# A four-layer convolution kernel on one core: keys transposed into single banks, four copies of x ahead of their products, the first load in halves, and layer 2's outputs of the second pair made two at a time

## The chip, the core and the metric

The kernel runs on one core of one Trainium2 chip, in one launch. The metric is the device time of that launch in microseconds; the median of several runs counts. TensorE (PE) multiplies matrices and writes into PSUM, which has eight banks of 128 partitions by 512 float32 values. VectorE (DVE) and ScalarE (ACT) work on what lies in PSUM and in the on-chip memory, GpSimd (POOL) does little here, and SyncE (SP) issues nearly all transfers (DMA). Each engine works through its own list in order, and semaphores make one engine wait for another.

## The reference

Input x has the shape (4, 512, 64, 64) in float32; four layers follow each other. Cut to what matters:

```python
# layer 0: attention over the 4096 places, 64 channels wide
t = einsum('oc,bchw->bohw', w_qkv, x)          # key, query, value: 64 rows each
attn = softmax(einsum('bdk,bdq->bkq', key, query), axis=1)
x = scale * einsum('oc,bchw->bohw', w_out, value @ attn) + x
# layer 1: three convolutions (1x1, 3x3, 1x1) with weights mixed from 8 experts, relu, plus x
# layer 2: linear attention
Q, K = softplus(Wq x + bq), softplus(Wk x + bk)          # 64 features at each place
KV = einsum('bmn,bcn->bmc', K, Wv x + bv)
norm = 1 / einsum('bnm,bm->bn', Q, K.sum(-1) + EPS)
x = x + gamma * einsum('bnm,bmc,bn->bcn', Q, KV, norm)
# layer 3: two 1x1 projections; one is summed with a discount along rows and columns
x = x + gamma * x_gate * sigmoid(cumsum(cumsum(x_scan, rows), columns))
```

## The kernel before

The four batches run one after the other, and within a batch the layers. A batch's x (512 channels, 4096 places) lies in four "pairs" of 1024 places (two blocks of 512), each a tile of 128 partitions by 4 groups of channels by 1024. PE's order is the program's order; DVE's and ACT's order is partly written by hand too (`manual_schedule`). PSUM is shared out by two pools: `pair_psum` gives two banks as one tile and has three such places, `bank` gives a single bank and has two. A tile can be written when the tile that stood in its place before has been read.

A float32 matmul shows as two records in the trace. Products with 64 rows or 64 columns of weights are issued for both halves of a pair, and their records run side by side.

**Start.** `load_pair` (line 87) loads the first batch's x on SP's queue, one transfer of 512 KB for each group of channels; the weights of layer 0's projections (`wqkv_sb`, line 99) come in two halves, one on ACT's queue, one first on SP's (line 102). Meanwhile PE makes two products of the identity with itself, the step "zero" (lines 305 to 310), and then the first products of x (`vv`, line 269), both halves of the pair.

**Layer 2.** `features` makes the key's features, `softplus` turns them into keys (logarithm on ACT, lines 701 to 717 on DVE). `key_transpose` (line 720) turns two pairs' keys by eight transposes into one `pair_psum` tile (`ktr`) and copies it with one instruction (`kt`, line 726). `move` (line 743) turns a quarter of a pair's x by eight transposes (`xtr`, line 748) and copies it out (`xt`, line 750) on ACT or DVE; `products` (line 755) multiplies keys and x into `g` (line 761). For the first pair the order is: quarters 0 and 1 moved early, keys turned, quarters 2 and 3 moved, the products of quarters 0 and 1, two moves of the next pair, the products of quarters 2 and 3 (`split=True`). After the second pair's products comes `kfold` (line 886), which needs the sums of all keys.

**Layer 3.** A batch's eight blocks (a pair and half of the channels) are made from lists of steps (lines 1118 to 1140): "s5" and the like are PE products for the sums, "g5" for the gates of the block before, the other words are work of ACT and DVE. Among them stand the outputs of layer 2 for pairs 1 to 3, twelve of them, in a list `ys`: "y" makes the next one (`value_product`, line 926, two products of 64 rows, `wv` at line 930), "a" adds it to x on DVE (`value_add`, line 935). "q" takes the next piece of what is left of layer 2 for the last two pairs from the list `left`: features, the sums' product `den2` (line 856, a bank) with its reciprocal on DVE (line 859), and `divide` (line 862, PE line 866, DVE line 869).

Of the kernel before, what the change touches and what calls it, by code (L numbers as in the profile page):

```python
# [14 lines left out]
B, C, H, W = 4, 512, 64, 64  # L15
P = 128
HW = H * W
NB = 512
# [3 lines left out]
D = 64  # L22
NT = HW // P
TPB = NB // P
NPAIR = NBLK // 2
# [21 lines left out]
def unshifted(ctx: ExitStack, tc: tile.TileContext, fits, x, wqkv_t, wout_t, router_t,  # L47
# [38 lines left out]
    def load_pair(b, pr):  # L86
        if b and pr == NPAIR - 1:
            places[NPAIR - 1:] = places[NPAIR], places[NPAIR - 1]
        t = places[pr]
        src = x[b, :, pr * 2 * NB:(pr + 1) * 2 * NB].rearrange("(kc p) n -> p kc n", p=P)  # L90
        if b == 0:
            for kc in range(KC):
                nc.sync.dma_start(t[:, kc, :], src[:, kc, :])
        else:
            nc.sync.dma_start(t, src)
        return t
# [1 line left out]

    wqkv_sb = const.tile([P, KC, 3 * D], F32, tag="wqkv", name="wqkv_sb")

    for queue, k in ((nc.scalar, 0), (nc.sync, 2)):
        queue.dma_start(wqkv_sb[:, k:k + 2, :], wqkv_t[:, k:k + 2, :])
    prm_sb = const.tile([P, NPRM], F32, tag="prm", name="prm_sb")
    def col(i, n=1):
        return prm_sb[:, i:i + n]
# [113 lines left out]
    class Projections:  # L219
# [70 lines left out]
        def products(self, xs, pair, steps, key, qry, vt):  # L290
            y = zy = None
            e = {}

            def to_key(src, pr, own=True):
                for h in range(2):
                    n0 = (2 * pr + h) * NB
                    for to in range(2):
                        if own or to != h:
                            nc.scalar.copy(key[to * D:(to + 1) * D, n0:n0 + NB], src(h, n0))

            for step in steps:
                step, _, channels = step.partition(":")
                if y is None and (step.isdigit() or step == "zero"):
                    y, zy = bank(f"kq_{self.b}_{pair[0]}"), pair_psum(f"kqz_{self.b}_{pair[0]}")
                if step == "zero":


                    for _ in range(2):
                        nc.tensor.matmul(zy[:, 0, :].rearrange("p (j c) -> p j c", c=P), ident,
                                         ident[:, None, :].to_broadcast([P, TPB, P]), start=True, stop=True)  # L310
                elif step.isdigit():
                    k = int(step)
                    to = y if k in (1, 6, 7, 4) else zy[:, 0 if k == 2 else 1, :]
                    for c in (int(channels),) if channels else range(2):
                        for h in range(2):
                            nc.tensor.matmul(to[h * D:(h + 1) * D, :], self.w[k][:, c, :],  # L316
                                             self.term(xs, pair, k, c)[:, h * NB:(h + 1) * NB],
                                             start=c == 0 and k in (1, 5), stop=c == 1,
                                             skip_group_check=k not in (1, 5))
                elif step == "roots":  # L320
                    norm_roots()
                elif step == "factors":
                    norm_factors()
                elif step == "seed":
                    nc.scalar.copy(zy[:, 0, :], y)
                elif step in ("e2", "e3"):
                    e[step] = block(f"{step}_{self.b}_{pair[0]}")
                    nc.scalar.copy(e[step], y)
                elif step == "c11":
                    to_key(lambda h, n0: zy[h * D:(h + 1) * D, 0, :], pair[0])  # L330
                elif step == "c12":
                    for h in range(2):
                        r, n0 = slice(h * D, (h + 1) * D), (2 * pair[1] + h) * NB
                        nc.vector.tensor_tensor(key[r, n0:n0 + NB], zy[r, 1, :], e["e2"][r, :], ALU.add)
                    self.left.append(lambda: to_key(lambda h, n0: key[h * D:(h + 1) * D, n0:n0 + NB], pair[1],
                                                    own=False))
                elif step == "k":
                    self.key_copies()
                elif step == "c21":
                    nc.vector.tensor_copy(qry[:, pair[0] * NB:(pair[0] + 1) * NB], y)  # L340
                elif step == "c22":
                    nc.vector.tensor_tensor(qry[:, pair[1] * NB:(pair[1] + 1) * NB], zy[:, 1, :], e["e3"], ALU.add)
                elif step[0] in "tn" and step[1].isdigit():
# [326 lines left out]
    def layer2(b, xs, sums_of_six, mix_last, conv2, conv3, wcq, qs):  # L670
# [47 lines left out]
                    kts[w, pr] = None  # L718

        def key_transpose(pair):  # L720
            ktr = pair_psum(f"ktr_{b}_{pair[0]}")
            for i, pr in enumerate(pair):
                for j in range(TPB):
                    nc.tensor.transpose(ktr[:, i, j * P:(j + 1) * P], kts[1, pr][:, j * P:(j + 1) * P], ident)
            kt = four(f"kt_{b}_{pair[0]}")
            nc.vector.tensor_copy(kt, ktr)
            for i, pr in enumerate(pair):
                kts[pr] = kt[:, i, :].rearrange("p (j c) -> p j c", c=P)

# [13 lines left out]
        def move(pr, j):  # L743
# [3 lines left out]
                for kc in range(KC):  # L747
                    nc.tensor.transpose(xtr[:, h, kc * P:(kc + 1) * P], xs[pr][:, kc, n0:n0 + P], ident)  # L748
# [6 lines left out]
        def products(pr, more=range(TPB), between=None, split=False):  # L755
            def multiply(js):
                for j in js:
                    t = pr * TPB + j
                    xt = moved.pop(0)
                    for h in range(2):  # L760
                        nc.tensor.matmul(g[h * D:(h + 1) * D, :], kts[pr][:, j, h * D:(h + 1) * D], xt[:, h, :],  # L761
                                         start=t == 0, stop=t == NPAIR * TPB - 1)
# [197 lines left out]
    def layer3(b, xs, value_product, value_add, left, weights, wcq):  # L960
# [109 lines left out]
        class Gates(Block):  # L1070
# [32 lines left out]
            def add_x(self, i, h=None):  # L1103
# [37 lines left out]
        with tc.manual_schedule(engines={mybir.EngineType.DVE, mybir.EngineType.Activation}):  # L1141
# [9 lines left out]
            for i in range(len(tiles) + 1):  # L1151
                who = {"l": last, "s": Sums(1, i) if i < len(tiles) else None, "g": Gates(0, i - 1) if i else None}
                if b == B - 1 and i >= len(tiles) - 1:
# [1 line left out]
                        break  # L1155
                    who["h"] = Gates(0, i)
                    who["h"].last = True
                made = None
                for step in first_steps if i == 0 else end_steps if "h" in who else steps if who["s"] else last_steps:
                    for what in step:  # L1160
                        name, *args = what.split()
# [3 lines left out]
                        elif name in who:  # L1165
                            if who[name]:
                                getattr(who[name], args[0])(*[int(a) for a in args[1:]])
                        elif name == "y":
                            if ys:
                                made = ys.pop(0)  # L1170
                                y = value_product(*made)
                        elif name == "a":
                            if made:
                                value_add(*made, y)
                                made = None
# [487 lines left out]
```

## Time and profile before

| | |
|---|---|
| median of 5 runs | 2639.87 us (2639.17 to 2640.45) |
| the profiled execution: time, span from first to last instruction | 2640.41 us, 2638.6 us |
| busy: DVE, ACT, POOL | 2066.2, 1320.5, 12.7 us |
| granted TensorE clock, mean | 0.999 |
| PE's share of the chain that ended last | 98% |
| DMA, mean over the span | 44 GB/s |

A row of the timeline gives the start, the duration, the engine, the line, what is written from what, the shapes, how many equal instructions are merged in the row, and in brackets how long the engine had been idle and what ended that. Since a matmul's end is modelled, starts are compared rather than durations. A row of the chain of waits gives the start, the time that the piece takes on the chain, and what it is.

### The profile page before, as it was taken

To read this page: it belongs to the slowest core of one execution; us is meant where nothing else is said; L and a number is where in the kernel's file an instruction comes from. 1 tells how busy PE (TensorE), PEld (TensorE's weight loads), DVE (VectorE), ACT (ScalarE), POOL (GpSimd) and SP (SyncE) were. 2 spreads that over 40 slices of the span, in tenths; PEclk is the share of its full clock that TensorE was granted. 3 is DMA by queue.
4 is the path that set the end of the run, shared out by engine and by line. 5 is a ranking of instruction groups with operands and counts; after the bars stand their busy time and mean duration, and the time that the engine had idled before them with its cause. 6 is when DMAs were issued, how large, how long until landed. Compare 5 with 4: busy or idle time off the path is not lost.

```text
span 2638.6 us, 25820 instructions
## 1 busy us (share of the span) xinstructions
PE 2626.3 (100%) x10018; PEld 1115.6 (42%) x10018; DVE 2066.2 (78%) x2332; ACT 1320.5 (50%) x1523; POOL 12.7 (0%) x26
## 2 busy tenths in 40 slices
PE   9999999999999999999999999999999999999998
PEld 3333455344333345444433334544443333554443
DVE  7777876888777787688877778768887777876887
ACT  4564353454555436345556553635555555263545
POOL 1000000000000000000000000000000000000000
PEclk9999999999999999999999999999999999999999
DMA  5000210022200021012220002101121000210001
GB/s 194 1 1 1 104 32 1 30 97 80 80 0 1 1 104 32 1 50 78 80 80 1 1 1 104 32 0 64 64 86 74 1 1 12 93 33 1 32 40 57
DMA packets 34739, 115.16 MB, mean 44 GB/s; under 512 B 3120, under 2 KB 12080, under 8 KB 33072
## 3 DMA queue, kind: packets, MB, share of 16 engines
q1 hardware_dynamic: 34464, 113.23, 11.4%
q8 instruction: 80, 1.31, 0.2%
q14 instruction: 51, 0.42, 0.1%
q10 hardware_dynamic: 144, 0.20, 0.0%
HBM read 79.86 MB, written 33.55 MB: 43 GB/s over the span
## 4 chain that ended last, share of the span: by engine, by line
PE 98%; DVE 1%; DMA 0%; ACT 0%; issue 0%; SPq 0%; ACTq 0%
PE av L399 17%; PE s L384 17%; PE sx L1012 16%; PE zy L1012 12%; PE c L657 4%; PE c L585 4%; PE c L634 3%; PE wv L930 3%; PE y L443 2%; PE g L761 2%; PE vv L269 2%; PE z L682 2%; PE kq L316 2%; PE xtr L748 2%; PE kqz L316 2%; PE c2e L634 2%
## 5 line engine op out<-in xcount | busy, mean ns | idle before, releaser
L384 PE MATMUL s<-qv,key 64*128 64x512 f32 x2048 | 454.0, 593 | 0.0
L387 ACT ACTIVATE ring<-s 128x1024 f32<-128x1024 f32 x336 | 315.4, 1053 | 249.9 <-PE s L384 249.9
L392 DVE TENSOR_TENSOR acc<-acc,ring 128x1024 f32<-128x1024 f32 x312 | 381.6, 1223 | 50.5 <-ACT ring L387 21.9
L399 PE MATMUL av<-ring,qv 128*64 128x512 f32 x1344 | 301.5, 595 | 0.0
L384 PEld LDWEIGHTS s<-qv,key 64*128 64x128 f32 x2048 | 192.7, 186 | 254.0 <-issue 112.4
L1012 PE MATMUL sx<-t,x 128*128 128x512 f32 x512 | 232.4, 594 | 0.0
L392 DVE TENSOR_TENSOR acc<-acc,x 128x1024 f32<-128x1024 f32 x168 | 205.5, 1223 | 32.4 <-ACT x L387 16.6
L387 ACT ACTIVATE x<-s 128x1024 f32<-128x1024 f32 x176 | 166.8, 1056 | 127.3 <-PE s L384 127.3
L399 PEld LDWEIGHTS av<-ring,qv 128*64 128x64 f32 x1344 | 92.6, 137 | 200.1 <-issue 200.1
L1017 ACT COPY zy<-sx 128x512 f32<-128x512 f32 x64 | 36.5, 570 | 253.9 <-PE sx L1012 253.9
L399 PE MATMUL av<-x,qv 128*64 128x512 f32 x704 | 159.5, 595 | 0.0
L1062 DVE TENSOR_TENSOR_SCAN t<-x,t 128x512 f32<-128x512 f32 x128 | 149.2, 1209 | 1.6
L1012 PEld LDWEIGHTS sx<-t,x 128*128 128x128 f32 x512 | 96.7, 190 | 124.6 <-issue 120.7
L1021 ACT ACTIVATE e<-sx,prm_sb 128x512 f32<-128x512 f32 x128 | 87.8, 686 | 122.2 <-PE sx L1012 122.2
L1045 DVE TENSOR_TENSOR_SCAN s<-wc,s 128x512 f32<-128x512 f32 x128 | 146.0, 1202 | 0.0
L1051 ACT COPY t<-s 128x1024 f32<-128x1024 f32 x64 | 127.5, 1992 | 29.2 <-DVE s L1045 28.7
L1068 ACT ACTIVATE s<-t 128x1024 f32<-128x1024 f32 x64 | 125.8, 1991 | 11.2 <-DVE t L1062 11.1
L1012 PE MATMUL zy<-t,wq 128*128 128x512 f32 x256 | 118.5, 602 | 0.0
L1012 PE MATMUL zy<-x,wq 128*128 128x512 f32 x256 | 118.0, 600 | 0.0
L1012 PE MATMUL sx<-x,wq 128*128 128x512 f32 x256 | 117.1, 595 | 0.0
L1012 PE MATMUL sx<-t,wq 128*128 128x512 f32 x256 | 116.6, 595 | 0.0
L1012 PE MATMUL zy<-x,x 128*128 128x512 f32 x256 | 116.3, 594 | 0.0
(262 smaller groups left out, 3506.4 us busy)
## 6 DMA issues: line engine op xcount, KB each, us to landing
out_dram<-s SPq DMA_DIRECT2D x62, 512.0 KB, 2.6
x<-in_x_dram SPq DMA_DIRECT2D x12, 2048.0 KB, 8.6
x<-in_x_dram SPq DMA_DIRECT2D x16, 512.0 KB, 9.1
ex<-in_packed_dram SPq DMA_DIRECT2D x4, 2048.0 KB, 8.2
ex<-in_experts_dram SPq DMA_DIRECT2D x4, 2048.0 KB, 7.7
wq<-in_wproj_t_dram SPq DMA_DIRECT2D x32, 256.0 KB, 4.7
ex<-in_packed_dram SPq DMA_DIRECT2D x4, 1536.0 KB, 6.0
ex<-in_experts_dram SPq DMA_DIRECT2D x4, 1536.0 KB, 6.4
```

The source lines that it names most:

```text
L316: nc.tensor.matmul(to[h * D:(h + 1) * D, :], self.w[k][:, c, :], self.term(xs, pair, k, c)[:, h * NB:(h + 1) * NB], start=c == 0 and k in ...
L384: nc.tensor.matmul(s[:, h, :], key[r, kt * P:(kt + 1) * P], qry[r, pr * NB:(pr + 1) * NB], start=True, stop=True)
L387: nc.scalar.activation(p, s, AF.Exp)
L392: nc.vector.tensor_tensor(accs[pr], accs[pr], p, ALU.add)
L399: nc.tensor.matmul(avs[pr][h * D:(h + 1) * D, :], vt[:, kt, :], ring[i % RING][:, h, :], start=kt == 0, stop=kt == NT - 1)
L585: nc.tensor.matmul(y[:, h, :], wc[:, kc, :], xs[pr][:, kc, h * NB:(h + 1) * NB], start=kc == 0, stop=kc == KC - 1)
L634: nc.tensor.matmul(y[:, lo - a:hi - a], u, v[:, lo:hi], start=dy == 1, stop=dy == 2)
L1012: nc.tensor.matmul(y, w[:, c, self.kind, self.j * P:(self.j + 1) * P], v[:, c, :], start=c == 0 and k in (1, 5), stop=c == 1, skip_group_c ...
L1045: nc.vector.tensor_tensor_scan(self.half(i, h), along[:, self.j + 2 * i, :], self.half(i, h), 0.0, ALU.mult, ALU.add)
L1051: nc.scalar.copy(self.t[i].rearrange("p (w r) -> p w r", w=W), self.s[i].rearrange("p (r w) -> p w r", w=W))
L1062: nc.vector.tensor_tensor_scan(th, down[:, i, :], th, 0.0, ALU.mult, ALU.add)
L1068: nc.scalar.activation(self.s[i].rearrange("p (r w) -> p w r", w=W), tw, AF.Sigmoid)
```

## The change

Four things are changed.

- Start: the first x transfer is split into two halves by columns and goes first on SP's queue; the second half of the weights follows it. The first of the two products of the identity is half as wide.
- Keys of the first two pairs: each is turned into a single bank and copied out by an instruction of its own.
- x of the first pair: quarters 2 and 3 are moved, then all four quarters are multiplied, then the second pair's four quarters are moved and multiplied. `g` takes its bank after the keys. The copies of quarter 3 (pair 0) and quarter 2 (pair 1) change places between ACT and DVE.
- Layer 3's first block: "y" becomes "yy", two outputs in a row, at two places, so that all four outputs of pair 1 are made there. Later blocks draw from the same list, and an output of pair 2 or 3 isn't made while `left` holds anything.

```diff
@@ load_pair
-                nc.sync.dma_start(t[:, kc, :], src[:, kc, :])
+                if (pr, kc) == (0, 0):
+                    for h in range(2):
+                        nc.sync.dma_start(t[:, kc, h * NB:(h + 1) * NB], src[:, kc, h * NB:(h + 1) * NB])
+                    nc.sync.dma_start(wqkv_sb[:, 2:4, :], wqkv_t[:, 2:4, :])
+                else:
+                    nc.sync.dma_start(t[:, kc, :], src[:, kc, :])
...
-    for queue, k in ((nc.scalar, 0), (nc.sync, 2)):
-        queue.dma_start(wqkv_sb[:, k:k + 2, :], wqkv_t[:, k:k + 2, :])
+    nc.scalar.dma_start(wqkv_sb[:, 0:2, :], wqkv_t[:, 0:2, :])
@@ step "zero"
-                    for _ in range(2):
-                        nc.tensor.matmul(zy[:, 0, :].rearrange("p (j c) -> p j c", c=P), ident,
-                                         ident[:, None, :].to_broadcast([P, TPB, P]), start=True, stop=True)
+                    for n in (TPB // 2, TPB):
+                        nc.tensor.matmul(zy[:, 0, 0:n * P].rearrange("p (j c) -> p j c", c=P), ident,
+                                         ident[:, None, :].to_broadcast([P, n, P]), start=True, stop=True)
@@ key_transpose
-            ktr = pair_psum(f"ktr_{b}_{pair[0]}")
+            if pair[0] == 0:
+                ktr = [bank(f"ktr_{b}_{pr}") for pr in pair]
+            else:
+                ktr = pair_psum(f"ktr_{b}_{pair[0]}")
...
-            nc.vector.tensor_copy(kt, ktr)
+            if pair[0] == 0:
+                for i in range(2):
+                    nc.vector.tensor_copy(kt[:, i, :], ktr[i])
+            else:
+                nc.vector.tensor_copy(kt, ktr)
@@ move
-            (nc.scalar.copy if j % 2 or (pr > 1 and j) else nc.vector.tensor_copy)(xt, xtr)
+            (nc.scalar.copy if pr and j else nc.vector.tensor_copy)(xt, xtr)
@@ products
-            if split:
-                multiply((0, 1))
-                for j in range(2):
-                    move(pr + 1, j)
-                multiply((2, 3))
-            else:
-                multiply(range(TPB))
+            for j in range(TPB):
+                t = pr * TPB + j
+                xt = moved.pop(0)
...
@@ layer 2, first two pairs
-            g = bank(f"g_{b}", (P, C))
             last_keys = features(1, (2, 3))
             keys()
             rest()
             key_transpose((0, 1))
+            g = bank(f"g_{b}", (P, C))
             move(0, 2)
+            move(0, 3)
             keys = last_keys()
-            products(0, (3,), split=True)
-            keys()
-            products(1, (2, 3))
+            products(0, ())
+            products(1, between=keys)
@@ layer 3
-                       ("s7", "s copy_out 3", "s fourth", "y"), ("s4", "s third", "a", "d"), ("y", "a", "q"),
+                       ("s7", "s copy_out 3", "s fourth", "yy"), ("s4", "s third", "a", "d", "a"), ("yy", "a", "a", "q"),
...
-                            if ys:
-                                made = ys.pop(0)
-                                y = value_product(*made)
+                            while ys and len(made) < len(name) and not (ys[0][0] > 1 and left):
+                                at = ys.pop(0)
+                                made.append((*at, value_product(*at)))
...
-                                value_add(*made, y)
-                                made = None
+                                value_add(*made.pop(0))
```

More of the change, by code (lines that the diff above doesn't have):

```diff
@@ L720, in key_transpose @@
         def key_transpose(pair):
-            ktr = pair_psum(f"ktr_{b}_{pair[0]}")
+            if pair[0] == 0:
+                ktr = [bank(f"ktr_{b}_{pr}") for pr in pair]
+            else:
+                ktr = pair_psum(f"ktr_{b}_{pair[0]}")
             for i, pr in enumerate(pair):
                 for j in range(TPB):
-                    nc.tensor.transpose(ktr[:, i, j * P:(j + 1) * P], kts[1, pr][:, j * P:(j + 1) * P], ident)
+                    to = ktr[i] if pair[0] == 0 else ktr[:, i]
+                    nc.tensor.transpose(to[:, j * P:(j + 1) * P], kts[1, pr][:, j * P:(j + 1) * P], ident)
             kt = four(f"kt_{b}_{pair[0]}")
-            nc.vector.tensor_copy(kt, ktr)
+            if pair[0] == 0:
[3 more added lines that the diff above has]
+                nc.vector.tensor_copy(kt, ktr)
             for i, pr in enumerate(pair):
@@ L749, in move, with products @@
             xt = four(f"xt_{b}_{pr}_{j}")
-            (nc.scalar.copy if j % 2 or (pr > 1 and j) else nc.vector.tensor_copy)(xt, xtr)
+            (nc.scalar.copy if pr and j else nc.vector.tensor_copy)(xt, xtr)
             moved.append(xt)
[L755 to L762, printed above, removed]
+        def products(pr, more=range(TPB), between=None):
             for j in more:
@@ L768, in products @@
                     between = None
-            if split:
-                multiply((0, 1))
-                for j in range(2):
-                    move(pr + 1, j)
-                multiply((2, 3))
-            else:
-                multiply(range(TPB))
+            for j in range(TPB):
+                t = pr * TPB + j
+                xt = moved.pop(0)
+                for h in range(2):
+                    nc.tensor.matmul(g[h * D:(h + 1) * D, :], kts[pr][:, j, h * D:(h + 1) * D], xt[:, h, :],
+                                     start=t == 0, stop=t == NPAIR * TPB - 1)
         with tc.manual_schedule(engines={mybir.EngineType.DVE}):
@@ L1157, in layer3 @@
                     who["h"].last = True
-                made = None
+                made = []
                 for step in first_steps if i == 0 else end_steps if "h" in who else steps if who["s"] else last_steps:
@@ L1167, in layer3 @@
                                 getattr(who[name], args[0])(*[int(a) for a in args[1:]])
-                        elif name == "y":
-                            if ys:
-                                made = ys.pop(0)
-                                y = value_product(*made)
+                        elif name in ("y", "yy"):
+                            while ys and len(made) < len(name) and not (ys[0][0] > 1 and left):
+                                at = ys.pop(0)
+                                made.append((*at, value_product(*at)))
                         elif name == "a":
                             if made:
-                                value_add(*made, y)
-                                made = None
+                                value_add(*made.pop(0))
                         elif name == "q":
```

## The prediction

> **What bounds the kernel.** The page first: PE is taken to be busy over the whole span, and the chain that ended last is 98% PE.
>
> ```profile
> PE 2626.3 (100%) x10018; PEld 1115.6 (42%) x10018; DVE 2066.2 (78%) x2332; ACT 1320.5 (50%) x1523; POOL 12.7 (0%) x26
> ```
>
> So only what takes time out of PE's own list counts. The waits of PE alone show how little there is to be had by waiting less:
>
> ```profile
> PE xtr L748 <- DVE kt L726: 1.8, 4, 0.4
> ...
> PE vv L269 <- DMA x<-in_x_dram: 0.2, 1, 0.2
> ```
>
> The first is one wait in each batch, at the place that the change rebuilds. But a busy PE isn't one at its pace. The chain in order of time, layer 3, first batch:
>
> ```profile
> 565.80 6.87 PE sx L1012 x16
> 592.35 6.87 PE sx L1012 x16
> 616.38 6.87 PE sx L1012 x16
> ```
>
> Sixteen records take 6.87 us, so 0.43 each. A block with two outputs of layer 2 in it takes 592.35 - 565.80 = 26.55 us, one without 616.38 - 592.35 = 24.03. An output thus costs (26.55 - 24.03) / 2 = 1.26 us. Its four records run two by two, 2 x 0.43 = 0.86 us, so 0.40 us goes into leaving the 128-row products and coming back. The chain of the first block shows where:
>
> ```profile
> 462.56 1.91 PE sx L1012 x4
> 464.47 1.06 PE wv L930 x4
> 465.53 0.98 PE den L856 x4
> 466.51 1.91 PE zy L1012 x4
> ```
>
> The output takes 1.06 instead of 0.86, and four records right after one take 1.91 instead of 1.72. Two outputs in a row take 1.92 (at 444.95 in the same view), that is 1.72 + 0.20: the second costs its 0.86 alone. Now layer 2, PE's timeline (start, duration):
>
> ```profile
> 405.05 1.04 PE L748 MATMUL xtr<-ident,x 128*128 128x128 f32 x8
> 406.53 1.09 PE L748 MATMUL xtr<-ident,x 128*128 128x128 f32 x8 [0.45 <-DVE kt L726]
> 407.55 1.94 PE L761 MATMUL g<-xt,kt 128*64 128x512 f32 x8
> 409.42 1.97 PE L748 MATMUL xtr<-ident,x 128*128 128x128 f32 x16
> 411.32 1.94 PE L761 MATMUL g<-xt,kt 128*64 128x512 f32 x8
> 413.18 1.97 PE L748 MATMUL xtr<-ident,x 128*128 128x128 f32 x16
> ```
>
> Quarter 3 of x starts 1.48 us after quarter 2, where eight transposes need half of 413.18's sixteen, 0.87 to 0.95: it waits for a place in PSUM that the keys hold until DVE's copy ends at 406.48. And the start:
>
> ```profile
> 1.46 3.78 PE L309 MATMUL kqz<-ident 128*128 128x512 f32 x4 [1.46 <-POOL ident masks.py:199]
> 5.43 1.97 PE L269 MATMUL vv<-x,wqkv_sb 128*64 128x512 f32 x4 [0.19 <-DMA x<-in_x_dram]
> 7.16 1.15 PE L316 MATMUL kq<-x,wqkv_sb 128*64 128x512 f32 x4
> ```
>
> Four records side by side take 1.73 us here and 0.86 from 8.13 on: PE runs at half pace until some 7.4 us.
>
> **Layer 2, the change costed.** Base: this execution's 2640.41 us (span 2638.6, 1.8 around it); the median of the runs, 2639.87, is 0.54 lower. The keys no longer hold a pair's place, and what stood in the three places before is read by then, so quarter 3 follows quarter 2 at 405.92. The keys' banks were last read by ACT's two half copies, done at 400.64, and `g` waits for the first keys' copy, which its products need anyway: both cost nothing. So the wait and its restart go, and the products start at 406.89 instead of 407.55: 0.66 gained. Not splitting removes one crossing into the 64-column products and back. Products and moves between 407.55 and 415.08 hold 16 records two by two (3.43) and 32 transposes at 0.109 (1.90 for sixteen at 413.18, less half a crossing; 3.49), 6.92 of 7.53, so two crossings cost 0.61 and one 0.30. Per batch 0.66 + 0.30 = 0.96, four times 3.85.
>
> What could take it back, step by step in before's clock. DVE is free of the query's features at 405.16; two copies of 0.69 (512 wide, as L713's and L340's rows) replace one of 1.23 and end at 405.9 and 406.5, so the products at 406.89 have their keys. DVE then copies quarter 2 to 407.7 and, new to it, quarter 3 to 408.85; the products ask for them at 408.7 and 409.5. Behind that copy stands L701, ending at 409.4 instead of 408.2, and behind it ACT's logarithm (408.24, now 409.5). Nobody misses it: the move of the next pair's first quarter starts at 410.47, its copy on DVE (1.13 after the start, as at 409.42 and 410.55) runs 411.6 to 412.85 and the fourth move, which takes its place, asks at 413.15. Then L708, L709 and two L713 follow as before (4.84 us from that copy's start to the last accumulation, 410.55 to 415.39) and end at 416.45. The products of the second pair run 414.1 to 417.6; `kfold` asks at 417.7. ACT, idle 2.24 and 1.78 us ahead of its copies, takes quarter 2 of the second pair; its last copy waits for L709 (415.1), ends at 416.15, and is asked for at 416.7. The smallest cover is 0.3 us. Bounds per batch: 1.0 if all holds, 0.35 if a new wait as long as the old one (0.6) appears; I take 0.96, since every step has cover.
>
> **Layer 3.** Before, block 0 and 1 hold four outputs in four crossings; after, [two], [two], and block 1 has one, since at its first "y" `left` still holds `divide`. The list then runs out in block 5 with one output instead of two. So twelve outputs cross 10 times, not 12: 2 x 0.40 = 0.80 us per batch without waits. But the second "yy" needs PSUM places that DVE frees by the first two adds. DVE's rows:
>
> ```profile
> 463.97 1.22 DVE L935 TENSOR_TENSOR x<-wv,x 128x1024 f32<-128x1024 f32 x1
> 465.58 1.22 DVE L935 TENSOR_TENSOR x<-wv,x 128x1024 f32<-128x1024 f32 x1 [0.39 <-PE wv L930]
> 466.72 3.34 DVE L859 RECIPROCAL inv<-den 64x512 f32<-64x512 f32 x1
> ```
>
> First pair 461.43 to 463.35 (1.92), "s4" 1.91, third output at 465.26: the first add ends at 465.19, just in time. The fourth output could start at 466.22; two adds in a row take 2.36 (at 446.06), so the second ends at 466.33: 0.16 late with its handover, and I add 0.10 for the restart, half of a crossing. Behind it `den2` moves from 465.46 to 467.43, and the reciprocal, which now follows two more adds, from 466.72 to 468.72, ending at 472.06. Before, block 1's first gate product waited for that bank (PE's next rows start at 468.26 and, eight records later, at 472.03: 3.77 where 3.44 + 0.09 is the pace, 0.24 lost); after, it could start at 471.95 and starts at 472.11, with its restart 0.26 lost, 0.03 with rounding more than before. DVE's next work (scans, 4.55 us) moves by 2.0 while PE moves by 0.8; the add that stood after the scans (1.19) is gone, and 2.45 us of DVE idle before L1076 covers the rest. Gain 0.80 - 0.26 - 0.03 = 0.51 per batch, 2.04 in all. Bounds: 0.80 without the wait, 0 if waits eat it; I take 0.51.
>
> **Start.** Half a product of the identity less is 0.86 us: PE is free at 4.4. The weights landed 3.4 us after their issue at 0.75, the first x (512 KB) 4.1 after 1.20, so 512 KB took 1.2 us behind the weights' 192. The first half (256 KB where 192 stood) lands at an estimated 4.3, the second 0.65 later at 4.95. One side of the products starts at 4.4, the other at 5.0, against 5.43; at half pace these 0.4 to 1.0 us are worth 0.2 to 0.5. I take 0.35. SP issues one more transfer (0.42), and the second pair's first x, ninth in line now, is issued only after a landing (4.1), which costs nothing while the four before it are still on their way (DVE's row at 11.04 is the first to use it); the later weights land at about 5.4; they are first read by PE at 10.7 and by DVE's short sums from 4.14 (2.6 us, ahead of idle until 11.04). DVE's first difference of x, whose halves end at 12.26 and 13.48, is asked for at 13.31 and 14.17, so up to 0.6 may be gained before it binds. Bounds: a gain of 0.9 if the pace rises earlier too; a loss of 3.0 if a pause before x makes PE start its 5.9 us of half pace again. I hold to the middle, since a pause of 0.19 did no harm.
>
> [...]
>
> **The sum.** 3.85 + 2.04 + 0.35 = 6.24 us: 2634.2 for the profiled execution, 2633.6 for the median.
>
> **Rivals.** (1) The pairs gain nothing: waits on the adds eat all. For it: the fourth output is late by my own count, and the third has only 0.05 in hand. Against it: one late start costs 0.26, and 0.80 is at stake. 2639.87 - 3.85 - 0.35 = 2635.7. (2) The pairs never wait: 2639.87 - 3.85 - 3.20 - 0.35 = 2632.5. For it: DVE's handovers are as short as 0.05. (3) The layer-2 part doesn't do what it says: the wait only moves, to quarter 3's copy or the fourth move (0.3 us of cover). Gain there 0.36 per batch: 2636.0. (4) The start loses its pace: 2633.6 + 0.35 + 3.0 = 2637.0. (5) Slower: DVE arrives late in layer 3's first block by the copy it took over (1.22) and puts both new adds (2.36) ahead of the reciprocal, on which the first gate product waits. Each batch loses 3.58 and gains 0.96 + 0.80: 4 x 1.82 - 0.35 = +6.9, 2646.8. It decides from a lateness of 1.6 us per batch on. Against it: DVE idles 6.62 us ahead of L918 and 1.50 ahead of L708, after which it runs in step with PE.
>
> **How the numbers follow.** A measurement of this kernel tells about 0.2%, 5.3 us, from no change. Forecast 0.60 (2633.0 to 2634.5), (2) 0.12: faster 0.72. (1) 0.13, (3) 0.06, (4) 0.03: within 0.2%, 0.22. (5) and its like 0.06. The range runs from 2631.7 (all upper bounds, 4.0 + 3.2 + 0.9 = 8.1) to 2637.0 (rival 4).
>
> **What would show it.** PE's wait on `kt` gone and `kfold` 0.96 us nearer to the keys' features; one row of 16 products for each pair; `wv` x8 in block 0 with at most one short wait before the fourth output; PE's first gate product after L859; block 5 1.26 us shorter; x products from 4.4 to 5.0. I am wrong if PE's waits name `xt`, L935 or L859 with more than 0.3 us per batch, or if the pace rises later than 7.4.

## The result and the profile after

The changed kernel takes 2634.10 us (median of 23 runs, 2633.01 to 2636.08); beside it on the same chips the kernel before takes 2639.69 us (43 runs, 2638.79 to 2641.64). That is 5.59 us less, a ratio of 0.9979 with a 95% interval of 0.9974 to 0.9985. The profiled execution took 2634.01 us, its span is 2632.2 us: 6.4 less than the span before.

The page of the changed kernel, busy time by engine, and all waits of PE that the trace lists (total in us, how often, longest). Most lines of the code are four further down than before (L1016 was L1012, L934 was L930), those of layer 2's transposes and products more (L733 was L724, L761 was L748, L778 was L761):

```profile
PE 2621.2 (100%) x10018; PEld 1117.0 (42%) x10018; DVE 2065.3 (78%) x2336; ACT 1321.1 (50%) x1523; POOL 12.1 (0%) x26
```

```profile
PE kqz L313 <- POOL ident masks.py:199: 1.5, 1, 1.5
PE vv L273 <- DMA x<-in_x_dram: 0.6, 1, 0.6
PE vv L273 <- DMA wqkv_sb<-in_wqkv_t_dram: 0.3, 1, 0.3
PE kqz L320 <- DVE ring L265: 0.2, 1, 0.2
```

The wait on `kt`, four times 0.45, is gone, and the list names no wait in its place in layers 1 to 3. What is new or longer in it lies in the first 15 us. DVE has four copies more (2336 instead of 2332), PE the same 10018 records.

PE's timeline in layer 2, first batch (start, duration, and so on, as before):

```profile
404.23 1.09 PE L733 MATMUL ktr<-ident,k 128*128 128x128 f32 x8
405.16 1.91 PE L761 MATMUL xtr<-ident,x 128*128 128x128 f32 x16
407.00 3.65 PE L778 MATMUL g<-xt,kt 128*64 128x512 f32 x16
410.58 3.71 PE L761 MATMUL xtr<-ident,x 128*128 128x128 f32 x32
414.22 3.65 PE L778 MATMUL g<-xt,kt 128*64 128x512 f32 x16
417.81 0.39 PE L890 MATMUL kfold<-ks,fold 128*128 128x4 f32 x2
```

Quarters 2 and 3 are one row of sixteen transposes without a pause, and each pair's products are one row of sixteen. From the first turned key to `kfold` it is 417.81 - 404.23 = 13.58 us; before it was 0.97 more, 418.67 - 404.12, by these two rows:

```profile
404.12 1.09 PE L724 MATMUL ktr<-ident,k 128*128 128x128 f32 x8
418.67 0.39 PE L886 MATMUL kfold<-ks,fold 128*128 128x4 f32 x2
```

The chain of waits in order of time (start, time on the chain, what), layer 3 of the first batch, its first block and the places where the blocks repeat:

```profile
460.64 1.92 PE wv L934 x8
462.56 1.91 PE sx L1016 x4
464.48 2.17 PE wv L934 x8
466.65 0.98 PE den L860 x4
...
565.69 6.87 PE sx L1016 x16
...
590.98 6.87 PE sx L1016 x16
...
615.01 6.87 PE sx L1016 x16
```

The first two outputs take 1.92 us and the second two 2.17: the fourth waited 0.25. The block from 565.69 to 590.98 takes 25.29 us with one output in it; before it was 26.55 with two.

Both traces laid side by side at the same rows of PE say where the time went. At the first key transposes of the batches the changed kernel is +0.11, -1.66, -3.15, -4.64 us against before; at `kfold` -0.86, -2.62, -4.11, -5.60; at PE's last product -6.12. So:

| part | forecast, us | in the profile, us |
|---|---|---|
| layer 2, four batches | -3.85 | -3.85 (-0.97, -0.96, -0.96, -0.96) |
| layer 3, four batches | -2.04 | -2.13 (-0.55, -0.53, -0.53, -0.52) |
| start, up to the first key transposes | -0.35 | +0.11 |
| layer 0 of the second batch | 0 | -0.25 |
| from the start of PE's last product to the end | 0 | -0.28 |
| sum | -6.24 | -6.4 |

The start went the wrong way in this pair of executions. PE's timeline there, then DVE's and PE's rows where DVE makes the first differences of x:

```profile
1.47 2.93 PE L313 MATMUL kqz<-ident 128*128 128x256 f32 x4 [1.47 <-POOL ident masks.py:199]
4.66 1.62 PE L273 MATMUL vv<-x,wqkv_sb 128*64 128x512 f32 x4 [0.26 <-DMA wqkv_sb<-in_wqkv_t_dram]
5.75 1.38 PE L320 MATMUL kq<-x,wqkv_sb 128*64 128x512 f32 x4
7.69 1.08 PE L273 MATMUL vv<-x,wqkv_sb 128*64 128x512 f32 x4 [0.56 <-DMA x<-in_x_dram]
...
12.95 1.08 PE L320 MATMUL kqz<-ring,wqkv_sb 128*64 128x512 f32 x4
14.23 1.08 PE L320 MATMUL kqz<-ring,wqkv_sb 128*64 128x512 f32 x4 [0.21 <-DVE ring L265]
```

```profile
11.67 2.51 DVE L265 TENSOR_TENSOR ring<-x,x 128x1024 f32<-128x1024 f32 x2 [3.31 <-DMA x<-in_x_dram]
```

PE began x's products at 4.66 instead of 5.43 and had full pace early (granted at 5.07 us; before at 7.38). PE didn't start when the first half of x had landed, at 4.42, but when the first half of the weights had, which came at 4.61 instead of 4.12. Then PE waits at 7.69 for x's second group, which landed at 7.65 (before 6.97), and at 14.23 for DVE, whose differences start when the second pair's first group has landed, at 11.64. Before, that group landed at 10.94:

```profile
11.04 2.44 DVE L261 TENSOR_TENSOR ring<-x,x 128x1024 f32<-128x1024 f32 x2 [4.28 <-DMA x<-in_x_dram]
```

### The profile page after: what moved, and what is told of

It is laid out like the page before. It is cut to its first block, busy times and chain, and to the rows that moved or that the text cites. A ratio compares the mean times of both kernels' runs of the same rounds, so it can differ in the third digit from the quotient of the medians.

```text
span 2632.2 us, 25829 instructions
## 1 busy us (share of the span) xinstructions
PE 2621.2 (100%) x10018; PEld 1117.0 (42%) x10018; DVE 2065.3 (78%) x2336; ACT 1321.1 (50%) x1523; POOL 12.1 (0%) x26
## 4 chain that ended last, share of the span: by engine, by line
PE 98%; DVE 1%; DMA 0%; ACT 0%; issue 0%; SPq 0%; ACTq 0%
PE av L403 17%; PE s L388 17%; PE sx L1016 16%; PE zy L1016 12%; PE c L661 4%; PE c L589 4%; PE c L638 3%; PE wv L934 2%; PE y L447 2%; PE g L778 2%; PE z L686 2%; PE xtr L761 2%; PE kq L320 2%; PE vv L273 2%; PE c2e L638 2%; PE kqz L320 1%
## 5 line engine op out<-in xcount | busy, mean ns | idle before, releaser
L1016 PE MATMUL sx<-t,x 128*128 128x512 f32 x512 | 232.4, 594 | 0.0
L1016 PEld LDWEIGHTS sx<-t,x 128*128 128x128 f32 x512 | 96.7, 190 | 124.6 <-issue 120.7
L1016 PE MATMUL zy<-t,wq 128*128 128x512 f32 x256 | 118.0, 601 | 0.0
L1016 PE MATMUL zy<-x,wq 128*128 128x512 f32 x256 | 117.6, 599 | 0.0
L1016 PE MATMUL sx<-x,wq 128*128 128x512 f32 x256 | 117.2, 595 | 0.0
L1016 PE MATMUL sx<-t,wq 128*128 128x512 f32 x256 | 116.6, 595 | 0.0
L1016 PE MATMUL zy<-x,x 128*128 128x512 f32 x256 | 116.3, 594 | 0.0
```

The lines of the kernel that those rows point to most:

```text
L1016: nc.tensor.matmul(y, w[:, c, self.kind, self.j * P:(self.j + 1) * P], v[:, c, :], start=c == 0 and k in (1, 5), stop=c == 1, skip_group_c ...
```

## The experiments

Kernels were timed in three groups, each on one chip with its own runs of the kernel before (medians 2639.81, 2640.28 and 2640.12 us): layer 2 alone, layer 3 alone, the start alone and all but the start; the reciprocal first, the keys in a pair's place and two halves of the start; the last four starts. "Position" is how much later than in the kernel before a batch's first key transpose starts in the profile.

**Layer 2 alone.** The diff's hunks of `key_transpose`, `move`, `products` and of the first two pairs, nothing else:

```diff
-            ktr = pair_psum(f"ktr_{b}_{pair[0]}")
+            if pair[0] == 0:
+                ktr = [bank(f"ktr_{b}_{pr}") for pr in pair]
...
-            products(0, (3,), split=True)
-            keys()
-            products(1, (2, 3))
+            products(0, ())
+            products(1, between=keys)
```

> The kernel before with the layer-2 part of the change alone (keys in single banks, x by four tiles). Theory (0.66 us of wait and 0.30 us of one crossing go in every batch, on their own): 4 x 0.96 = 3.85 us faster than before, about 2635.9; from the keys' transposes to kfold each batch 0.96 us shorter, everything else as before. Rival (the gain is bound up with the other parts, because the later work of DVE only fits when layer 3 is rearranged too): less than 3 us, with a new wait of PE in layer 3's first block.

2635.55 us (11 runs), 4.26 less, 0.9982 (0.9973 to 0.9992). In the trace `kfold` comes nearer to the key transposes by 0.97, 0.97, 0.97 and 0.96 us: 3.87. The part stands on its own; the rival falls.

**Layer 3 alone.**

```diff
-                       ("s7", "s copy_out 3", "s fourth", "y"), ("s4", "s third", "a", "d"), ("y", "a", "q"),
+                       ("s7", "s copy_out 3", "s fourth", "yy"), ("s4", "s third", "a", "d", "a"), ("yy", "a", "a", "q"),
...
```

> The kernel before with layer 3's outputs of the second pair by twos alone. Theory (two crossings of 0.40 us saved, 0.26 us given back at the fourth output): 0.53 us per batch, 2.1 us faster than before, about 2637.7, the second pair of outputs 0.25 us longer than the first. Rival 1 (in the changed kernel DVE was ahead thanks to layer 2; alone the adds eat all): 0 to 1 us. Rival 2 (alone DVE is earlier, because it copies one quarter of x less in layer 2, and the fourth output doesn't wait): 0.80 us per batch, 3.2 us, about 2636.6.

2637.35 us (11 runs), 2.46 less, 0.9991 (0.9982 to 1.0). The trace gains 0.53, 0.53, 0.52 and 0.52 in the four layers 3, 2.1 in all. PE's timeline of this kernel, first block:

```profile
460.78 1.99 PE L930 MATMUL wv<-wc,kv 64*128 64x512 f32 x8
462.70 1.98 PE L1012 MATMUL sx<-t,wq 128*128 128x512 f32 x4
464.61 2.24 PE L930 MATMUL wv<-wc,kv 64*128 64x512 f32 x8
466.79 1.05 PE L856 MATMUL den<-wc,kbd 128*32 128x512 f32 x4
```

The second two outputs take 466.79 - 464.61 = 2.18 us here too, the first 1.92: the fourth output's wait is one of this part's own, and neither rival holds.

**The start alone.** The hunks of `load_pair`, of `wqkv_sb` and of the step "zero":

```diff
-                nc.sync.dma_start(t[:, kc, :], src[:, kc, :])
+                if (pr, kc) == (0, 0):
+                    for h in range(2):
+                        nc.sync.dma_start(t[:, kc, h * NB:(h + 1) * NB], src[:, kc, h * NB:(h + 1) * NB])
+                    nc.sync.dma_start(wqkv_sb[:, 2:4, :], wqkv_t[:, 2:4, :])
...
-                    for _ in range(2):
+                    for n in (TPB // 2, TPB):
```

> The kernel before with the new order of loads and the shorter warm-up alone. Theory (the second half of the weights now stands ahead of x's second group on SP's queue, and every later group of x lands about 0.7 us later, which PE then waits for): 0.0 to 0.5 us slower than before, x's second group at about 7.6 us where it was at 7.0. The prediction's term: 0.35 us faster. Rival (the clock's rise decides and not the loads): the time goes with the moment at which full pace is granted, either way by up to 1 us, whatever the landings are.

2640.36 us (11 runs), 0.55 more, 1.0002 (0.9993 to 1.0011): no gain, as the theory had it (0.0 to 0.5 slower), and no loss that the interval tells from none. x's second group landed at 7.45. Its position is -0.09 although full pace came at 6.34, a microsecond earlier than in the kernel before; here the clock's rise by itself doesn't decide.

**All but the start.** The changed kernel with the old loads and the old warm-up.

```diff
-    nc.scalar.dma_start(wqkv_sb[:, 0:2, :], wqkv_t[:, 0:2, :])
+    for queue, k in ((nc.scalar, 0), (nc.sync, 2)):
+        queue.dma_start(wqkv_sb[:, k:k + 2, :], wqkv_t[:, k:k + 2, :])
...
-                    for n in (TPB // 2, TPB):
+                    for _ in range(2):
```

> The changed kernel with the old loads and the old warm-up: the two other parts together. Theory (the parts add up, and the start gave nothing): 3.85 + 2.1 = 6.0 us faster than before, about 2633.8, and within 0.5 us of the changed kernel. If the start had given its 0.35 us as forecast, this one would be 0.35 us slower than the changed kernel; if the late x costs, up to 0.5 us faster.

2633.37 us (9 runs), 6.44 less, 0.9975 (0.9966 to 0.9985). The two parts add up (4.26 + 2.46 = 6.72 alone), and without the start's edits the kernel is 0.85 further from its own runs of before than the whole change is from its own.

**Keys back in a pair's place,** x still by four tiles, old start.

```diff
-            if pair[0] == 0:
-                ktr = [bank(f"ktr_{b}_{pr}") for pr in pair]
-            else:
-                ktr = pair_psum(f"ktr_{b}_{pair[0]}")
+            ktr = pair_psum(f"ktr_{b}_{pair[0]}")
...
-            if pair[0] == 0:
-                for i in range(2):
-                    nc.vector.tensor_copy(kt[:, i, :], ktr[i])
-            else:
-                nc.vector.tensor_copy(kt, ktr)
+            nc.vector.tensor_copy(kt, ktr)
```

> The changed kernel without its start part, and with the first keys back in a pair's place in PSUM with one copy; x still moves by four tiles. Theory (the wait of 0.66 us came from the place that the keys held, the other 0.30 us from the split products): the wait on the keys' copy is back at 0.45 us in the rows and 0.6 to 0.7 us of PE per batch, so 2.4 to 2.8 us slower than the kernel with the keys in banks. Rival (moving all of x ahead of the products already hides the copy): within 0.5 us of it.

2636.90 us (11 runs), 3.38 less, 0.9989 (0.998 to 0.9998). PE's waits and its timeline in this kernel:

```profile
PE xtr L750 <- DVE kt L728: 1.8, 4, 0.4
```

```profile
404.75 1.04 PE L750 MATMUL xtr<-ident,x 128*128 128x128 f32 x8
406.23 1.09 PE L750 MATMUL xtr<-ident,x 128*128 128x128 f32 x8 [0.44 <-DVE kt L728]
407.25 3.65 PE L767 MATMUL g<-xt,kt 128*64 128x512 f32 x16
410.83 3.71 PE L750 MATMUL xtr<-ident,x 128*128 128x128 f32 x32
```

The wait is back exactly as it was. From the keys to `kfold` this kernel gains 0.30 us per batch where the banks bring 0.97: 0.66 belongs to the place that the keys held, 0.30 to the crossing saved. By the medians it is 3.06 behind the kernel with the keys in banks (3.38 against 6.44 less), more than the 2.4 to 2.8 that the theory gave: four times 0.66 is 2.65, and the second batch's layer 0, below, takes 0.25 more. The rival falls.

**The reciprocal first.** Old start; in layer 3's first block the fourth pair's denominators go ahead of the second two outputs.

```diff
-                       ("s7", "s copy_out 3", "s fourth", "yy"), ("s4", "s third", "a", "d", "a"), ("yy", "a", "a", "q"),
+                       ("s7", "s copy_out 3", "s fourth", "yy"), ("s4", "s third", "a", "d", "a"), ("q", "yy", "a", "a"),
```

> The changed kernel without its start part, and in layer 3's first block the fourth pair's denominators and their reciprocal ahead of the second pair of outputs. Theory (the fourth output waits 0.25 us for the second add, and the first gate product 0.24 us for the reciprocal that stands behind two adds; with the reciprocal first both go): 0.5 us per batch, 2.0 us faster than the same kernel with the reciprocal behind the outputs, about 7.8 us faster than before. Rival (DVE is then 3.34 us longer from the first adds to the second ones, and the places in PSUM that those hold are asked for): the waits only move, 0 to 1 us slower than with the reciprocal behind.

2631.81 us (6 runs), 8.47 less, 0.9968 (0.9956 to 0.998). PE's timeline, then DVE's:

```profile
460.24 1.99 PE L930 MATMUL wv<-wc,kv 64*128 64x512 f32 x8
462.16 1.98 PE L1012 MATMUL sx<-t,wq 128*128 128x512 f32 x4
464.07 1.05 PE L856 MATMUL den<-wc,kbd 128*32 128x512 f32 x4
465.05 1.99 PE L930 MATMUL wv<-wc,kv 64*128 64x512 f32 x8
466.97 1.98 PE L1012 MATMUL zy<-x,x 128*128 128x512 f32 x4
468.79 3.60 PE L1012 MATMUL sx<-x,wq 128*128 128x512 f32 x8
472.23 3.60 PE L1012 MATMUL zy<-t,wq 128*128 128x512 f32 x8
```

```profile
462.79 2.34 DVE L935 TENSOR_TENSOR x<-wv,x 128x1024 f32<-128x1024 f32 x2
465.20 3.35 DVE L859 RECIPROCAL inv<-den 64x512 f32<-64x512 f32 x1
468.47 2.28 DVE L935 TENSOR_TENSOR x<-wv,x 128x1024 f32<-128x1024 f32 x2
```

The second two outputs take 1.92 us now (465.05 to 466.97), and the gate products after them 3.44 (468.79 to 472.23) instead of 3.68 (469.39 to 473.07 in the changed kernel). Layer 3 gains 1.03 per batch over before where the change gains 0.53: 0.5 more, 2.0 in four, as the theory said. The second two adds end at 470.75, some 2.8 us later than in the changed kernel (467.94), and no wait of PE names them.

**Which half of the start.** The next two undo one half each: one has the old loads with the shorter warm-up, the other the new loads with the old warm-up.

```diff
@@ old loads, shorter warm-up: against the kernel without the start
-                    for _ in range(2):
+                    for n in (TPB // 2, TPB):
@@ new loads, old warm-up: against the changed kernel
-                    for n in (TPB // 2, TPB):
+                    for _ in range(2):
```

> The changed kernel with the old loads and the shorter warm-up. Theory (PE then only waits 0.86 us for x, which lands at the same time as before): within 0.2 us of the kernel with the old warm-up; x's groups land as in the kernel before (second group at about 7.0 us). Rival (a pause before x makes the half pace start anew): 1 to 3 us slower, with the clock granted later than 7.4 us.

> The changed kernel with the new loads and the old warm-up. Theory (the weights on SP's queue push x's groups back, and the warm-up has no part in it): second group of x at about 7.6 us, as in the changed kernel, and the time within 0.3 us of the changed kernel; against the kernel with old loads 0.1 to 0.5 us slower. Rival (the shorter warm-up is what lost the start): 0.3 to 0.5 us faster than the changed kernel.

The first: 2634.85 us (11 runs), 5.43 less, 0.9979 (0.997 to 0.9988). The second: 2633.64 us (10 runs), 6.64 less, 0.9975 (0.9965 to 0.9984). By the medians both theories fall: the shorter warm-up with old loads is 1.0 us worse than the old one, and the loads cost no time. The profile of the second shows the opposite, a position of +1.05; but its execution took 2635.34 us, the slowest of that kernel's ten, 1.7 above their median. Its start:

```profile
4.83 1.48 PE L273 MATMUL vv<-x,wqkv_sb 128*64 128x512 f32 x4
5.74 1.43 PE L320 MATMUL kq<-x,wqkv_sb 128*64 128x512 f32 x4
8.66 1.08 PE L273 MATMUL vv<-x,wqkv_sb 128*64 128x512 f32 x4 [1.50 <-DMA x<-in_x_dram]
```

PE had full pace at 4.42 us and then waited 1.50 for a group that landed at 8.62. And the first one's:

```profile
1.46 2.93 PE L309 MATMUL kqz<-ident 128*128 128x256 f32 x4 [1.46 <-POOL ident masks.py:199]
5.50 1.97 PE L269 MATMUL vv<-x,wqkv_sb 128*64 128x512 f32 x4 [1.11 <-DMA x<-in_x_dram]
7.23 1.91 PE L316 MATMUL kq<-x,wqkv_sb 128*64 128x512 f32 x4
8.94 1.06 PE L269 MATMUL vv<-x,wqkv_sb 128*64 128x512 f32 x4
```

Here x came at its usual time (PE starts on it at 5.50, before at 5.43), but two rows of four run at half pace, and full pace was granted only at 8.98. So one execution of a start says little. Four starts were then timed on one chip, all with the reciprocal first:

```diff
@@ A: two products; B has one and a half, as the change
-                    for n in (TPB // 2, TPB):
+                    for _ in range(2):
@@ C: one product
-                    for n in (TPB // 2, TPB):
+                    for _ in range(1):
@@ D: two products, the weights' second half on ACT's queue
-                    nc.sync.dma_start(wqkv_sb[:, 2:4, :], wqkv_t[:, 2:4, :])
...
     nc.scalar.dma_start(wqkv_sb[:, 0:2, :], wqkv_t[:, 0:2, :])
+    nc.scalar.dma_start(wqkv_sb[:, 2:4, :], wqkv_t[:, 2:4, :])
```

> The changed kernel with the fourth pair's reciprocal ahead of the second pair of outputs and with the old warm-up (two full products of the identity), the new loads kept. Theory (the warm-up that is half a product shorter lost about 1.0 us, the new order of loads alone gains about 0.2): 8.5 to 8.8 us faster than before, the fastest of the four kernels of this job or level with the one with the weights on ACT's queue. Rival (the starts only differ by chance): within 0.3 us of the same kernel with the shorter warm-up.

> The changed kernel with the fourth pair's reciprocal ahead of the second pair of outputs, its start as the change has it (one and a half products). Theory: 0.8 to 1.1 us slower than the same kernel with the old warm-up, about 7.6 us faster than before. Rival (chance): within 0.3 us.

> As the two kernels beside it, with a single product of the identity as warm-up. In the profiles with two products full pace was granted 2.9 to 6.0 us after PE's first row. Theory (a pause after a short warm-up makes that time begin again when x lands, at about 4.7 us, so the pace rises at 7.6 to 10.7 us instead of 4.4 to 7.5, and half of the 3.2 us is lost, less what PE would have waited for x's second group anyway): 1.0 to 1.6 us slower than with two products. Rival 1 (loss in proportion to the warm-up left out): 2.0 us slower, twice that of one and a half. Rival 2 (x's second group binds and not the pace): within 0.4 us.

> As the kernel with the old warm-up, but the weights' second half behind the first on ACT's queue instead of between x's transfers on SP's. Theory (the weights ahead of it push x's second group back: 7.45 to 8.62 us in three profiles, against 6.81 to 7.54 in seven with the old order): second group of x at 6.8 to 7.4 us, 0.2 to 0.8 us faster than the kernel with the weights on SP's queue. Rival (the same bytes go through the same transfer engines, in whichever queue they stand): second group as late as with SP's queue, and within 0.2 us.

A: 2631.80 us (6 runs), 0.9969 (0.9957 to 0.9981). B: 2632.32 (6 runs), 0.997 (0.9958 to 0.9983). C: 2632.61 (8 runs), 0.997 (0.996 to 0.9981). D: 2631.23 (6 runs), 0.9966 (0.9954 to 0.9979). A is 8.32 less than before, short of its theory's 8.5 to 8.8. With six runs that spread over 2 us, 0.5 between A and B is not told from chance; B's theory had 0.8 to 1.1. C loses 0.8, less than the theory's 1.0 to 1.6 and rival 1's 2.0, more than rival 2's 0.4. D is 0.57 better than A, as its theory had it, which the intervals don't tell from chance either; its second group of x landed at 7.27, but so did C's, at 7.29, with the weights on SP's queue.

Three pairs of kernels differ in the warm-up alone, by half a product, and three in the loads alone. How much less than their own runs of before they take, by the medians, in us:

| only this differs | old | new | new is slower by |
|---|---|---|---|
| warm-up, with old loads | 6.44 | 5.43 | 1.01 |
| warm-up, with new loads | 6.64 | 5.59 | 1.05 |
| warm-up, reciprocal first (A, B) | 8.32 | 7.80 | 0.52 |
| loads, with the old warm-up | 6.44 | 6.64 | -0.20 |
| loads, with the shorter warm-up | 5.43 | 5.59 | -0.16 |
| loads, reciprocal first (its first run above, and A) | 8.47 | 8.32 | 0.15 |

No pair by itself is told from chance by its intervals. But all three warm-ups point one way and the loads go both ways: over the runs the start's loss follows the shorter warm-up and not the new loads.

The profiles show what sets the start of a single execution, if all fourteen are put together. "Lands" is the second pair's first group of x, "full pace" the granted clock, "position" that of the first batch, all in us; 11.53 is fitted to the rows:

| start | lands | full pace | position | lands - 11.53 |
|---|---|---|---|---|
| before | 10.94 | 7.38 | 0 | -0.59 |
| layer 2 alone | 11.52 | 7.45 | +0.03 | -0.01 |
| layer 3 alone | 10.90 | 4.37 | -0.64 | -0.63 |
| all but the start | 11.30 | 6.87 | -0.20 | -0.23 |
| reciprocal first | 11.32 | 4.55 | -0.23 | -0.21 |
| keys in pair | 11.23 | 4.93 | -0.30 | -0.30 |
| old loads, short warm-up | 10.96 | 8.98 | +0.83 | -0.57 |
| the change | 11.64 | 5.07 | +0.11 | +0.11 |
| start alone | 11.45 | 6.34 | -0.09 | -0.08 |
| new loads, old warm-up | 12.59 | 4.42 | +1.05 | +1.06 |
| A | 11.78 | 6.27 | +0.24 | +0.25 |
| B | 11.79 | 4.99 | +0.24 | +0.26 |
| C | 11.31 | 10.09 | +1.26 | -0.22 |
| D | 11.26 | 4.34 | -0.27 | -0.27 |

In eleven of fourteen the position is the landing less 11.53, to within 0.04 us: DVE's differences start there, and PE follows DVE. In the other three full pace came late for their landing (7.38, 8.98 and 10.09), and the position is later than the landing gives; 7.45, with layer 2 alone, did no harm beside a landing of 11.52. The new loads land later: on average 11.76 in six profiles against 11.17 in the seven with the old ones, 0.59. Without the slow execution of the new loads with the old warm-up it is 11.59, 0.43 later. The kernel before is itself a late row: the five others with the old loads and the old warm-up lie at +0.03 to -0.64.

## Why the prediction was right, and where it was wrong

The time came out 0.5 us above the forecast, inside its own range of 2633.0 to 2634.5. Layers 2 and 3 gave what they should; the start gave nothing, and by the runs it cost 0.55 alone and 0.85 with the rest. That the profiled execution (2634.01) lies even 0.2 below its forecast is luck: 0.25 in layer 0 and 0.28 behind PE's last product were not forecast and cover the start. Point by point:

- **Layer 2** is right in mechanism and size: 0.66 + 0.30 = 0.96 forecast, 0.96 to 0.97 measured, and the kernel with the keys back in a pair's place shows both terms apart (0.66 and 0.30). The covers counted for DVE and ACT held: no wait on `xt`, `kt` or L701. Rival 3 falls.
- **Layer 3** is right as well: 0.51 forecast, 0.53 measured; two crossings of 0.40 less a wait. The fourth output lost 0.25 (forecast 0.26), and the block with one output instead of two is 26.55 - 25.29 = 1.26 shorter, the price of an output to the hundredth. Rivals 1 and 2 fall by the run with this part alone; the slower rival fell with them, since DVE was never late enough for a second wait. The first gate product still loses 0.24 to the reciprocal (3.68 instead of 3.44), as before, where 0.26 was forecast.
- **The start** is the step that failed: "One side of the products starts at 4.4, the other at 5.0, against 5.43; at half pace these 0.4 to 1.0 us are worth 0.2 to 0.5. I take 0.35." PE did start at 4.66, but the term valued PE's first products, while in the profiled execution the start is set by a later transfer. The step that let this pass is the one on the second pair's first x, "which costs nothing while the four before it are still on their way", together with DVE's differences, of which it said that "up to 0.6 may be gained before it binds". That 0.6 assumed the landing unmoved. It moved by 0.70 in the profile, so the cover became -0.1, and +0.11 is what was measured. Over the runs it is another term that fails, "Half a product of the identity less is 0.86 us: PE is free at 4.4", which counts the shorter warm-up as a gain: with everything else equal it was 0.52 to 1.05 slower, and the loads between 0.20 faster and 0.15 slower. How the shorter warm-up costs this in the changed kernel is not shown; its one profile has full pace early, at 5.07.
- **Rival 4** (the start loses its pace) happened, but not in the changed kernel's profile: with pauses of 1.11 and 1.19 us before x full pace came at 8.98 and 10.09, with pauses up to 0.34 ahead of it never after 7.45. Their positions, +0.83 and +1.26, are 1.40 and 1.48 above what their landings give (-0.57 and -0.22); in these two executions that, and not 3.0, was the price.
- **Not forecast:** 0.25 us in the second batch's layer 0. In the kernel before DVE stood still there for 0.46 us between two of the sums ahead of `den`, and PE's products behind `den` started 0.25 later. This pause is there in the kernel before, with layer 3 alone, with the start alone and with the keys in a pair's place, and in none of the ten kernels with the keys in banks. Why it goes with the banks was not found. Shifts of the same size come and go in layer 0 elsewhere: with the start alone the third and fourth batches began 0.10 and 0.23 later at their first `kqz` rows, where nothing was changed.

What stays open besides is why the new loads land later in the profiles. Between 2 and 7 us the seven profiles with the old order carried 1725 to 1825 KB, the six with halves first and the weights on SP's queue 1537 to 1680, and D, with the weights on ACT's queue, 1682. 160 KB less on average is 0.4 us at the 380 GB/s of those microseconds, which is the delay told in bytes and not its cause. Whether the halves or the queue do it, one profile of D doesn't tell, and in the run times the delay doesn't show.

The fastest kernel that ran is D: the change with the reciprocal ahead of the second two outputs and the weights on ACT's queue, 8.89 us below before. The reciprocal's 2.0 us are shown in the traces; what D's start adds isn't told from chance.

## What to carry to other kernels

When a first transfer is made smaller so that an engine can start sooner, look for the first consumer that waits for one of the transfers behind it: the gain is at most what that consumer gains, and a cover computed from the old landings is void if the edit moves them (here by 0.70 us in the profile). When a warm-up is shortened along with it, time the two apart. Where PE is full, count the crossings between shapes of products (here 0.40 us for each output made alone in layer 3, 0.30 for the one saved in layer 2) and group the products of one shape, then look at what the grouped consumers push back on the other engine: here the long reciprocal (3.35 us), moved ahead of them, gave as much again (0.50 us per batch) as the grouping (0.53). For a stage that varies between executions, look at many profiles and at the medians of all runs before naming a cause: here one profile blamed the loads and the runs the warm-up.

## What was unexpected of the hardware

Full pace lasted 2618.02, 2621.44, 2624.85 or 2628.26 us in the profiles, steps of 3.41 us. In twelve of the fourteen its start lay anywhere from 4.34 to 7.45 us with PE first busy at 1.46 or 1.47, in the other two at 8.98 and 10.09. In the stretch of 3.41 us that ended with the grant PE had idled at most 0.55 us (D, 0.92 to 4.34); stretches before it with 0.84 idle or more (layer 2 alone, 0.62 to 4.03; the old loads with the short warm-up, 2.16 to 5.57, with its pause of 1.11) brought no grant. So in these profiles the warm-up lost its effect where a pause of 1.11 or 1.19 us followed it: full pace came at 8.98 and 10.09. Why the lengths differ by whole steps, and what decides in which stretch the pace rises, these runs don't show.

The second pair's first group of x landed anywhere from 10.90 to 11.52 us under one and the same order of loads, and the time from the start of PE's last product to the end of the span ran from 8.43 to 9.55 us in no order of the edits. Each spread, 0.62 and 1.12, is about as large as the start's whole effect.
